# Subject residual: the run length of one of a slot's two loads, and the place of ScalarE's loop in the text

## The chip, the cores and the metric

The kernel runs on one core of one Trainium2 chip. The metric is device time in microseconds, the median of the runs of a kernel; smaller is better.

## The reference

Each of 128 samples x[b] (128 channels by 1024 steps, float32) is multiplied by the 128 by 128 matrix of its subject, one of eight, and added to itself:

```
w = weights[subjects]                      # (128, 128, 128), subjects in 0..7
out = einsum('bct,bcd->bdt', x, w)
x + out
```

x and the result have 67.1 MB each; the weights have 0.5 MB.

## The kernel before

The samples are worked in 32 turns (NT) of four: H = 2 halves of G = 2 samples. A turn has a *slot*, a piece of SBUF of 2 MB (128 partitions of 16 KB); there are 12 (SLOTS), used round robin. A slot is loaded, multiplied in place and stored from where it lies. The residual is in the weights: `place` (L193) adds the identity (`eye`) to the subject's matrix, so that one matmul gives x + out.

*Loads.* ScalarE issues two DMAs for a slot (`load`, L147), one for each half, 1 MB each. The source, two samples that lie one behind the other in HBM, is written as rows of ROWS channels: with ROWS = 8 a row is 8 x 1024 numbers, a run of 32 KB, and there are 32 of them. The destination is 128 partitions of 2048 numbers. Since source and destination are walked in the same flat order, partition p of a half gets channels 2(p mod 64) and 2(p mod 64) + 1 of sample p // 64, whatever ROWS is. Both samples of a half thus share a column range of the slot, one in the upper and one in the lower 64 partitions.

*Trades.* `trade` (L162) puts that right with three copies on ScalarE, each 64 partitions by 2048 numbers: after them each sample of the slot has all 128 partitions to itself, with two channels of it side by side in the partition order that the sorted weights and `eye` expect. The last copy of a slot raises `s_half[0]`, for which TensorE waits.

*ScalarE's loop* (L273) has AHEAD = 4 slots in a turn. For each it waits until the slot's two loads have landed (`landed`), then until a slot is empty (`s_empty`), issues the loads of the slot four ahead, and only then trades. So a trade stands behind the wait for an empty slot. Ahead of the loop ScalarE issues the loads of the first four slots (L268), loads its table and copies one element (`mark`, L271).

*Empty slots.* `s_empty` begins at SLOTS - 1 - AHEAD = 7, gets one more when the first product has been copied (the last slot holds the raw weights until then), and then one for each store that has landed, counted by GpSimd (L309).

*Multiplying.* For each half TensorE does four float32 matmuls of 128 x 128 by 512 (L206) into PSUM, VectorE copies the half back to the slot (`copy`, L221, 128 x 2048) and places the weights of the half two further on.

*Stores.* SyncE waits for VectorE's copies and stores the slot (`store`, L172), 2 MB a DMA; from slot 20 on two slots share a DMA of 4 MB. The runs of the first store are 4 KB, those of the next ones 16 KB (a partition's part of a slot), and 32 KB for the last six slots. After its last store the program ends when that has landed.

*Where the text stands.* Each engine runs its own instructions in the order in which the text gives them to it. A loop opens a new block, to which engines with work behind it branch. In the kernel before, ScalarE's loop is written ahead of the second half of the weights' sorting (VectorE and GpSimd, L293 to L305), GpSimd's counting, SyncE's stores (L311) and the loops of VectorE (L330) and TensorE (L336).

Of the kernel before, what the change touches and what calls it, by code (L numbers as in the profile page):

```python
# [30 lines left out]
G = 2  # L31
H = 2
# [3 lines left out]
SLOTS = 12  # L36
# [9 lines left out]

IDLE = 8

ROWS = 8

R = 2

AHEAD = 4

MOVES = 3
# [9 lines left out]
def transfer(nc, engine, out, in_):  # L65

    later, nc._always_lower_symbolic_ap = nc._always_lower_symbolic_ap, False
    ins, outs = engine.lower_ap_dma(in_), engine.lower_ap_dma(out)  # L70
    nc._always_lower_symbolic_ap = later
    return engine.add_instruction(
        mybir.InstDMACopy(
            name=nc.get_next_instruction_name(),
            engine=engine.engine,
            ins=ins,
            outs=outs,
            mode="Copy",
            cce_op=ALU.bypass,
            queue=QUEUES[engine.engine],  # L80
        )
    )
# [3 lines left out]
def kernel(  # L86
# [7 lines left out]
    nc = tc.nc  # L94
    B, C, T = x.shape
    S, _, D = weights.shape
    NT = B // (G * H)

    def sbuf(name, *shape, dtype=F32):
        return ctx.enter_context(nc.sbuf_tensor(name, list(shape), dtype)).ap()  # L100
# [3 lines left out]
    eye = sbuf("eye", C, 1, D)  # L104
    ws = [sbuf(f"w{i}", C, 1, D) for i in range(G)]
    mark = sbuf("mark", 1, 1)
# [32 lines left out]
    s_eye = tc.alloc_semaphore("s_eye")  # L139
    s_moved = tc.alloc_semaphore("s_moved")  # L140
    s_empty = tc.alloc_semaphore("s_empty")
    s_sort = tc.alloc_semaphore("s_sort")

    def emptied(i):
        return DMA * (i // SLOTS)

    def load(k, slot, first):  # L147
        for h in range(H):
            transfer(
                nc,  # L150
                nc.scalar,
                x_all[:, bass.ds(slot * (H * G * T) + h * G * T, G * T)],
                x[bass.ds(first + h * G, G)].rearrange("h (b r) t -> (h b) (r t)", r=ROWS),
            ).then_inc(s_in[k], DMA)

    def move(out, in_):
        nc.scalar.copy(out, in_).then_inc(s_moved, 1)  # L157

    def landed(k):
        nc.scalar.wait_ge(s_in[k], DMA * H).then_inc(s_in[k], -DMA * H)  # L160

    def trade(k, slot):  # L162
        base = slot * (H * G * T)
        both = x_all[:, bass.ds(base, H * G * T)].rearrange("c (h s t) -> c s h t", h=H, s=G)
        move(aside, both[A:, 0])
        nc.scalar.wait_ge(s_moved, k * MOVES + 1)
        move(both[A:, 0], both[:A, 1])
        nc.scalar.wait_ge(s_moved, k * MOVES + 2)
        move(both[:A, 1], aside)
        nc.scalar.wait_ge(s_moved, (k + 1) * MOVES).then_inc(s_half[0], 1)  # L170
# [52 lines left out]
    with tc.tile_critical():  # L223

        nc.sync.dma_start(
            w_raw, weights.rearrange("s (u j) d -> (s u) (j d)", j=S)
        ).then_inc(s_wall, DMA)
        nc.sync.dma_start(given, subjects.rearrange("(o b) -> o b", o=1)).then_inc(s_given, DMA)

        nc.vector.memset(zeros, 0.0).then_inc(s_zeros, 1)  # L230
        nc.tensor.wait_ge(s_zeros, 1)
        for _ in range(IDLE):
            nc.tensor.matmul(  # L233
                ps[P_SLOTS - 1][:, G - 1, :N], zeros[:, :D], zeros, start=True, stop=True
            )

        nc.vector.wait_ge(s_wall, DMA)  # L240
        for r in range(R):
            nc.vector.transpose(  # L242
                w_mid.rearrange("p (e r h w j) -> p r j h e w", e=4, r=R, h=4, w=8)[:, r],
                w_raw.rearrange("p (j r d) -> p r j d", r=R, d=D)[:, r],
            ).then_inc(s_sort, 1)
        nc.vector.memset(index[:, B:], 0).then_inc(s_index, 1)
        nc.vector.wait_ge(s_given, DMA)
        nc.vector.tensor_scalar(near, given, -S, S - 1, ALU.max, ALU.min).then_inc(s_index, 1)  # L248
        nc.vector.wait_ge(s_index, 2)
        nc.vector.tensor_scalar(wrap, near, 0, S, ALU.is_lt, ALU.mult).then_inc(s_index, 1)  # L250
        nc.vector.wait_ge(s_index, 3)
        nc.vector.tensor_tensor(index[:, :B], near, wrap, ALU.add).then_inc(s_index, 1)  # L252

        nc.gpsimd.wait_ge(s_zeros, 1)
        for r in range(R):
            if r:
                nc.gpsimd.wait_ge(s_eye, r)
            nc.gpsimd.affine_select(  # L258
                eye[:, 0],
                eye[:, 0] if r else zeros[:, :D],  # L260
                [[-1, D]],
                ALU.not_equal,
                1.0,
                base=r - r * R * A,
                channel_multiplier=R,
            ).then_inc(s_eye, 1)

        for i in range(AHEAD):  # L268
            load(i % AHEAD, i, i * (H * G))
        nc.scalar.wait_ge(s_eye, R)  # L270
        nc.scalar.copy(mark, eye[:1, 0, :1])  # L271
        nc.gpsimd.wait_ge(s_eye, R).then_inc(s_empty, SLOTS - 1 - AHEAD)
        with nc.scalar.Fori(0, NT // AHEAD) as turn:  # L273
            for k in range(AHEAD):
                landed(k)
                with nc.scalar.If(turn < NT // AHEAD - 1):
                    empty = nc.scalar.wait_ge(s_empty, k + 1)
                    if k + 1 == AHEAD:
                        empty.then_inc(s_empty, -AHEAD)
                    load(  # L280
                        k,
                        (turn * AHEAD + (k + AHEAD)) % SLOTS,
                        nc.s_assert_within(
                            turn * (AHEAD * H * G) + (k + AHEAD) * H * G,
                            0,
                            B - H * G,
                            skip_runtime_bounds_check_because="the last turn loads nothing",
                        ),
                    )
                trade(k, (turn * AHEAD + k) % SLOTS)  # L290
            nc.scalar.wait_ge(s_moved, AHEAD * MOVES).then_inc(s_moved, -AHEAD * MOVES)

        nc.vector.wait_ge(s_sort, R)  # L293
        nc.vector.transpose(w_late, w_mid).then_inc(s_sort, 1)  # L294

        def sort(engine, o, v):
            engine.tensor_copy(  # L297
                w_all[32 * v : 32 * (v + 1), 2 * o : 2 * (o + 1), :],
                w_late[32 * o : 32 * (o + 1)].rearrange(
                    "c (e u r d) -> c u r e d", e=2, u=2, r=R  # L300
                )[:, v % 2, v // 2],
            ).then_inc(s_sort, 1)

        nc.vector.wait_ge(s_sort, R + 1)
        nc.gpsimd.wait_ge(s_sort, R + 1)  # L305
        for o in range(4):
            for v in range(4):
                sort(nc.gpsimd if v == 3 else nc.vector, o, v)
        nc.gpsimd.wait_ge(s_added, 1).then_inc(s_empty, 1)  # L309
        for i in range(SLOTS, NT):  # L310
            nc.gpsimd.wait_ge(s_slot[i % SLOTS], emptied(i)).then_inc(s_empty, 1)  # L311

        for i in [*range(NT - SLOTS), *range(NT - SLOTS, NT, PAIR)]:
            n = 1 if i < NT - SLOTS else PAIR
            nc.sync.wait_ge(s_added, (i + n) * H)
            if i == 0:
                nc.sync.dma_start(
                    out[: H * G].rearrange("g d t -> d g t"), xs[0]
                ).then_inc(s_slot[0], DMA)
            elif i + n < NT:  # L320
                store(i, n).then_inc(s_slot[i % SLOTS], DMA)


        nc.vector.wait_ge(s_index, 4)
        nc.vector.wait_ge(s_sort, SORTED)
        nc.vector.wait_ge(s_eye, R)
        subject = subjects_of(slice(0, H * G))
        for h in range(H):
            place(h, subject)
        with nc.vector.Fori(0, NT // TURN) as turn:  # L330
            for n in range(TURN):
                subject = subjects_of(turn * TURN + (n + 1))
                for h in range(H):
                    copy((turn * TURN + n) % SLOTS, n, h)
                    place(h, subject)
        with nc.tensor.Fori(0, NT) as turn:  # L336
            for h in range(H):
                multiply(turn % SLOTS, h)

    with tc.tile_critical() as waits:  # L340
        for i in range(NT - SLOTS, NT - PAIR, PAIR):
            nc.scalar.wait_ge(s_slot[i % SLOTS], emptied(i + SLOTS))
    last = store(NT - PAIR, PAIR)
# [34 lines left out]
```

## Time and profile before

| | us |
|---|---|
| median of 3 runs | 322.94 |
| the three runs | 322.62 to 323.04 |
| the profiled execution | 323.06 |
| its span, first to last instruction | 321.2 |
| PE busy | 250.1 |
| ScalarE busy | 183.6 |
| VectorE busy | 181.4 |

The profiled execution agrees with the runs within 0.1 us. The profile counts DMA as packets in queues: q1 is SyncE's (the stores, the weights, the subjects), q10 is ScalarE's (the loads of x). A queue's share is the time of its packets over the 16 DMA engines' span, so the shares of the queues add up to how busy the engines were. A queue's packets include small ones under 512 B that carry nothing of x: 16 close each DMA.

### The profile page before, as it was taken

To read this page: it belongs to the slowest core of one execution; us is meant where nothing else is said; L and a number is where in the kernel's file an instruction comes from. 1 tells how busy PE (TensorE), PEld (TensorE's weight loads), DVE (VectorE), ACT (ScalarE), POOL (GpSimd) and SP (SyncE) were. 2 spreads that over 40 slices of the span, in tenths; PEclk is the share of its full clock that TensorE was granted. 3 is DMA by queue.
4 is the path that set the end of the run, shared out by engine and by line. 5 is a ranking of instruction groups with operands and counts; after the bars stand their busy time and mean duration, and the time that the engine had idled before them with its cause. 6 is when DMAs were issued, how large, how long until landed. Compare 5 with 4: busy or idle time off the path is not lost. (4 is left out here: it accounts for less than half of the span.)

```text
span 321.2 us, 2576 instructions
## 1 busy us (share of the span) xinstructions
PE 250.1 (78%) x528; PEld 103.4 (32%) x528; DVE 181.4 (56%) x217; ACT 183.6 (57%) x98; POOL 2.5 (1%) x10
## 2 busy tenths in 40 slices
PE   7479998898899885949987499673997939999400
PEld 3134433333333332413433143231433414444100
DVE  4708766666677662660865627456273753877600
ACT  1577767776777726566454774547746379990000
POOL 0200000000000000000000000000000000000000
PEclk9969999999999997995999979998697998999955
DMA  8999999999999999999999999999999999999995
GB/s 314 404 457 424 420 403 436 408 433 445 426 424 426 435 414 430 437 430 441 433 402 426 416 433 441 428 418 422 426 439 441 408 453 408 426 445 418 433 428 228
DMA packets 7732, 134.76 MB, mean 420 GB/s; under 512 B 1457, under 2 KB 1458, under 8 KB 2098
## 3 DMA queue, kind: packets, MB, share of 16 engines
q1 hardware_dynamic: 4658, 67.64, 49.9%
q10 hardware_dynamic: 3072, 67.11, 49.0%
q14 instruction: 2, 0.02, 0.0%
HBM read 67.63 MB, written 67.11 MB: 419 GB/s over the span
## 5 line engine op out<-in xcount | busy, mean ns | idle before, releaser
L206 PE MATMUL ps<-x_all,w 128*128 x512 | 239.9, 627 | 48.7 <-PEq L202 48.7
L221 DVE COPY x_all<-ps 128x2048 f32 x64 | 146.6, 2291 | 116.1 <-PE ps L206 103.5
L206 PEld LDWEIGHTS ps<-x_all,w 128*128 128x128 f32 x512 | 99.3, 200 | 189.3 <-issue 189.2
L157 ACT COPY aside<-x_all 64x2048 f32 x32 | 60.7, 1897 | 95.0 <-issue 90.6
L157 ACT COPY x_all<-x_all x32 | 60.7, 1897 | 4.0
L157 ACT COPY x_all<-aside 64x2048 f32 x32 | 60.7, 1898 | 1.0
L195 DVE TENSOR_TENSOR w<-w_all,eye 128x128 f32<-128x128 f32 x132 | 31.8, 282 | 0.8 <-issue 0.8
L233 PE MATMUL ps<-x_all 128*128 128x512 f32 x16 | 10.2, 808 | 1.7 <-DVE x_all L230 1.7
L233 PEld LDWEIGHTS ps<-x_all 128*128 128x128 f32 x16 | 4.1, 262 | 6.9 <-issue 5.3
L271 ACT ACT_TABLE_LOAD x1 | 1.3, 1283 | 6.1 <-issue 6.1
L297 DVE COPY w_all<-x_all 32x256 f32<-32x256 f32 x12 | 3.9, 326 | 0.4
L242 DVE STREAM_TRANSPOSE x_all<-x_all 128x512 f32<-128x512 f32 x2 | 2.0, 1068 | 3.2 <-DMA x_all<-in_L_cond_weights_dram 3.2
L297 POOL COPY w_all<-x_all 32x256 f32<-32x256 f32 x4 | 1.7, 424 | 6.7 <-DVE x_all L294 6.6
L294 DVE STREAM_TRANSPOSE x_all<-x_all 128x1024 f32<-128x1024 f32 x1 | 1.2, 1226 | 0.0
L230 DVE MEMSET x_all<- 128x512 f32 x1 | 0.5, 485 | 1.0 <-SPq L223 1.0
L248 DVE TENSOR_SCALAR x_all<-x_all 1x128 int32<-1x128 int32 x1 | 0.2, 217 | 0.3 <-DMA x_all<-in_itok_B_dram 0.3
L258 POOL TENSOR_SCALAR_AFFINE_SELECT eye<-x_all 128x128 f32<-128x128 f32 x1 | 0.3, 292 | 1.4 <-DVE x_all L230 1.4
L252 DVE CUSTOM_DVE_ANT_0 index<-x_all 1x256 uint16<-1x256 uint16 x1 | 0.3, 280 | 0.0
L258 POOL TENSOR_SCALAR_AFFINE_SELECT eye<-eye 128x128 f32<-128x128 f32 x1 | 0.3, 292 | 0.1
L250 DVE TENSOR_SCALAR x_all<-x_all 1x128 int32<-1x128 int32 x1 | 0.2, 215 | 0.0
L271 ACT COPY mark<-eye 1x1 f32<-1x1 f32 x1 | 0.2, 190 | 0.0
L365 POOL MEMSET const-bfloat16-1.0<- 128x1 bf16 x1 | 0.1, 100 | 0.0
(5 smaller groups left out, 0.4 us busy)
## 6 DMA issues: line engine op xcount, KB each, us to landing
x_all<-in_x_dram ACTq DMA_DIRECT2D x64, 1024.0 KB, 11.6
out_dram<-x_all SPq DMA_DIRECT2D x20, 2048.0 KB, 55.0
out_dram<-x_all SPq DMA_DIRECT2D x6, 4096.0 KB, 30.9
x_all<-in_L_cond_weights_dram SPq DMA_DIRECT2D x1, 512.0 KB, 3.9
x_all<-in_itok_B_dram SPq DMA_DIRECT2D x1, 0.5 KB
```

The source lines that it names most:

```text
L157: nc.scalar.copy(out, in_).then_inc(s_moved, 1)
L195: copy = nc.vector.tensor_tensor(ws[q], w_all[:, bass.ds(subject[q], 1), :], eye, ALU.add)
L206: mm = nc.tensor.matmul(ps[h][:, q % G, t : t + N], ws[q][:, 0, :], x_all[:, bass.ds(at, N)], start=True, stop=True,)
L221: nc.vector.tensor_copy(mine, ps[h].rearrange("d g t -> d (g t)")).then_inc(s_added, 1)
L230: nc.vector.memset(zeros, 0.0).then_inc(s_zeros, 1)
L233: nc.tensor.matmul(ps[P_SLOTS - 1][:, G - 1, :N], zeros[:, :D], zeros, start=True, stop=True)
L242: nc.vector.transpose(w_mid.rearrange("p (e r h w j) -> p r j h e w", e=4, r=R, h=4, w=8)[:, r], w_raw.rearrange("p (j r d) -> p r j d", r ...
L252: nc.vector.tensor_tensor(index[:, :B], near, wrap, ALU.add).then_inc(s_index, 1)
L258: nc.gpsimd.affine_select(eye[:, 0], eye[:, 0] if r else zeros[:, :D], [[-1, D]], ALU.not_equal, 1.0, base=r - r * R * A, channel_multipli ...
L271: nc.scalar.copy(mark, eye[:1, 0, :1])
L294: nc.vector.transpose(w_late, w_mid).then_inc(s_sort, 1)
L297: engine.tensor_copy(w_all[32 * v : 32 * (v + 1), 2 * o : 2 * (o + 1), :], w_late[32 * o : 32 * (o + 1)].rearrange("c (e u r d) -> c u r e ...
```

## The change

Two edits. First, ROWS becomes a list: the load of the first half of a slot is written as 64 rows of 4 channels (16 KB runs), that of the second half as 32 rows of 8 channels (32 KB runs), as both were. Bytes, destinations, issue order and semaphores are as before.

Second, what ScalarE does after the first loads (its wait for `eye`, the copy of `mark`, its loop) is written last, behind the rest of the sorting, GpSimd's counting, SyncE's stores and the loops of VectorE and TensorE. No other line changes.

```
-ROWS = 8
+ROWS = [4, 8]
...
-                x[bass.ds(first + h * G, G)].rearrange("h (b r) t -> (h b) (r t)", r=ROWS),
+                x[bass.ds(first + h * G, G)].rearrange("h (b r) t -> (h b) (r t)", r=ROWS[h]),
             ).then_inc(s_in[k], DMA)
...
         for i in range(AHEAD):
             load(i % AHEAD, i, i * (H * G))
+        nc.gpsimd.wait_ge(s_eye, R).then_inc(s_empty, SLOTS - 1 - AHEAD)
+        nc.vector.wait_ge(s_sort, R)
+        nc.vector.transpose(w_late, w_mid).then_inc(s_sort, 1)
...
+        with nc.tensor.Fori(0, NT) as turn:
+            for h in range(H):
+                multiply(turn % SLOTS, h)
+
         nc.scalar.wait_ge(s_eye, R)
         nc.scalar.copy(mark, eye[:1, 0, :1])
-        nc.gpsimd.wait_ge(s_eye, R).then_inc(s_empty, SLOTS - 1 - AHEAD)
         with nc.scalar.Fori(0, NT // AHEAD) as turn:
             for k in range(AHEAD):
                 landed(k)
```

What the second edit moves is seen in the order of each engine's instructions. On ScalarE (ACT), from its start to the first loads of the loop; `L72` are the loads, `mark` is the one element copied after the table load:

```order
 L374 UNCONDITIONAL_BRANCH x2
 L72 DMA x_all<-in_x_dram 128x2048 x8
-L271 ACT_TABLE_LOAD
-L271 COPY mark<-eye 1x1
-L273 UNCONDITIONAL_BRANCH
-L276 COMPARE_AND_BRANCH
+L225 UNCONDITIONAL_BRANCH
+L319 ACT_TABLE_LOAD
+L319 COPY mark<-eye 1x1
+L320 UNCONDITIONAL_BRANCH
+L323 COMPARE_AND_BRANCH
 L70 ISA x2
```

A branch to the block with the loop stands ahead of the table load now; the rest of ScalarE's instructions keep their order, under other line numbers.

On VectorE (DVE), between the subjects' index and the sorting of the weights:

```order
 L250 TENSOR_SCALAR x_all<-x_all 1x128
 L252 ISA index<-x_all 1x256
-L225 UNCONDITIONAL_BRANCH
-L294 STREAM_TRANSPOSE x_all<-x_all 128x1024
-L297 COPY w_all<-x_all 32x256 x12
+L272 STREAM_TRANSPOSE x_all<-x_all 128x1024
+L275 COPY w_all<-x_all 32x256 x12
 L184 TENSOR_LOAD index
```

The branch ahead of the transposition is gone.

On SyncE (SP), from the load of the subjects to the last but one store:

```order
 L228 DMA x_all<-in_itok_B_7_dram 1x128
-L225 UNCONDITIONAL_BRANCH
-L317 DMA out_dram<-x_all 128x4x1024
+L295 DMA out_dram<-x_all 128x4x1024
 L72 DMA out_dram<-x_all 128x4x1024 x19
 L72 DMA out_dram<-x_all 128x8x1024 x5
-L293 UNCONDITIONAL_BRANCH
+L225 UNCONDITIONAL_BRANCH
```

Of its two branches the one ahead of the stores is gone, and one behind them stays.

More of the change, by code (lines that the diff above doesn't have):

```diff
@@ L269 @@
             load(i % AHEAD, i, i * (H * G))
-        nc.scalar.wait_ge(s_eye, R)
-        nc.scalar.copy(mark, eye[:1, 0, :1])
         nc.gpsimd.wait_ge(s_eye, R).then_inc(s_empty, SLOTS - 1 - AHEAD)
[L273 to L291, printed above, removed]
         nc.vector.wait_ge(s_sort, R)
@@ L338 @@
                 multiply(turn % SLOTS, h)
+        nc.scalar.wait_ge(s_eye, R)
+        nc.scalar.copy(mark, eye[:1, 0, :1])
+        with nc.scalar.Fori(0, NT // AHEAD) as turn:
+            for k in range(AHEAD):
+                landed(k)
+                with nc.scalar.If(turn < NT // AHEAD - 1):
+                    empty = nc.scalar.wait_ge(s_empty, k + 1)
+                    if k + 1 == AHEAD:
+                        empty.then_inc(s_empty, -AHEAD)
+                    load(
+                        k,
+                        (turn * AHEAD + (k + AHEAD)) % SLOTS,
+                        nc.s_assert_within(
+                            turn * (AHEAD * H * G) + (k + AHEAD) * H * G,
+                            0,
+                            B - H * G,
+                            skip_runtime_bounds_check_because="the last turn loads nothing",
+                        ),
+                    )
+                trade(k, (turn * AHEAD + k) % SLOTS)
+            nc.scalar.wait_ge(s_moved, AHEAD * MOVES).then_inc(s_moved, -AHEAD * MOVES)
     with tc.tile_critical() as waits:
```

## The prediction

> **What bounds the kernel now.** I read the page's head and its DMA rows first, because the kernel reads and writes all of x once and computes little. The rows are the span, the DMA engines' busy share in 40 slices, the bytes moved, and the two queues (q10 carries the loads that ScalarE issues, q1 carries SyncE's stores and the two small loads at the start).
>
> ```profile
> span 321.2 us, 2576 instructions
> PE 250.1 (78%) x528; PEld 103.4 (32%) x528; DVE 181.4 (56%) x217; ACT 183.6 (57%) x98; POOL 2.5 (1%) x10
> DMA  8999999999999999999999999999999999999995
> GB/s 314 404 457 424 420 403 436 408 433 445 426 424 426 435 414 430 437 430 441 433 402 426 416 433 441 428 418 422 426 439 441 408 453 408 426 445 418 433 428 228
> DMA packets 7732, 134.76 MB, mean 420 GB/s; under 512 B 1457, under 2 KB 1458, under 8 KB 2098
> q1 hardware_dynamic: 4658, 67.64, 49.9%
> q10 hardware_dynamic: 3072, 67.11, 49.0%
> ```
>
> Packets take 49.9% + 49.0% = 98.9% of 16 engines' span, 317.7 of 321.2 us. No compute engine comes near that (PE 78%). So the DMA engines are the bound from the first slice to the last, and a wait between compute engines is worth nothing unless it leaves both queues empty. Next I read stretches of the span, and in three of them the queues' own rows: 10 to 28 us has only loads, 270 to 288 us only stores in 16 KB runs, 291 to 316 us only stores in 32 KB runs. The last two columns of the first fence are DMA share and GB/s.
>
> ```profile
> 10.00:28.00 18.00, 12.14 (x25) 5.02 (x24) 7.84 (x18) 12.57 (x7) 0.91 (x3) 0.81 1.01 435
> 30.00:56.00 26.00, 24.42 (x57) 10.15 (x56) 18.84 (x21) 18.83 (x11) 0.00 (x0) 1.00 1.00 415
> 56.00:116.00 60.00, 54.11 (x122) 22.52 (x122) 40.35 (x45) 40.72 (x22) 0.00 (x0) 1.00 1.00 429
> 116.00:268.00 152.00, 116.61 (x238) 47.87 (x237) 80.72 (x90) 88.55 (x47) 0.00 (x0) 0.91 1.00 427
> 270.00:288.00 18.00, 18.00 (x43) 7.62 (x42) 14.11 (x16) 15.93 (x10) 0.00 (x0) 1.00 1.00 424
> ```
>
> ```profile
> DMA packets 351, 7.83 MB, mean 435 GB/s; under 512 B 112, under 2 KB 112, under 8 KB 112
> q10 hardware_dynamic: 351, 7.83, 101.2%
> ```
>
> ```profile
> DMA packets 483, 7.64 MB, mean 424 GB/s; under 512 B 17, under 2 KB 17, under 8 KB 17
> q1 hardware_dynamic: 483, 7.64, 99.8%
> ```
>
> ```profile
> DMA packets 360, 10.75 MB, mean 430 GB/s; under 512 B 32, under 2 KB 32, under 8 KB 32
> q1 hardware_dynamic: 360, 10.75, 100.8%
> out_dram<-x_all SPq DMA_DIRECT2D x1, 4096.0 KB, 16.5
> ```
>
> The share is 1.00 in every stretch. Taking the packets under 512 B away (they carry no data of x), a 32 KB load packet takes 1.012 x 16 x 18 us / 239 = 1219.5 ns, a 16 KB store packet 0.998 x 288 us / 466 = 616.8 ns, a 32 KB store packet 1.008 x 400 us / 328 = 1229.3 ns. One packet split in two costs 2 x 616.8 - 1229.3 = 4.3 ns more.
>
> **Part 1, the 16 KB runs.** A load now has 32 packets of 32 KB; the first load of each slot gets 64 of 16 KB. That is 32 slots x 32 = 1024 packets more, 64 for each of 16 engines. No row shows a 16 KB load, so I bound its price. The nearest row is the split of a store: 64 x 4.3 ns = 0.28 us. The far row is what a load packet costs beyond its 1219.5 ns when stores run beside it, over the long middle and, without pauses of the loads, over its first part (60 to 260 us, then 60 to 100 us):
>
> ```profile
> q10 hardware_dynamic: 2040, 44.34, 51.9%
> q1 hardware_dynamic: 2824, 41.29, 48.7%
> ```
>
> ```profile
> q10 hardware_dynamic: 475, 10.36, 60.4%
> q1 hardware_dynamic: 472, 6.95, 40.8%
> ```
>
> 44.34 MB are 1353 packets, and 0.519 x 3200 us / 1353 = 1227.5 ns, 8.0 ns over. If every added packet met that as well, it would be 64 x (4.3 + 8.0) = 0.79 us. From below I can't exclude a gain, which the next step prices. I take 0.28 us, since it is the same size of packet on the same engines, and keep 0.79 us for the range.
>
> The Trainium skill, page DMA: Bandwidth & Descriptors, section Why small descriptors are slow (HBM only), gives a fixed cost of about 3 cycles a packet; at the 850 MHz of its section Where 436 GB/s comes from I estimate 3.5 ns, and by that the sum would be 64 x 3.5 = 0.23 us, without the far end. The trace agrees for stores alone (4.3 ns) and not for loads beside stores (8.0 ns over).
>
> **What the runs do to the two queues' shares.** Two places: 221 to 227 us, where both queues have work, and 176 to 180 us.
>
> ```profile
> q10 hardware_dynamic: 61, 1.47, 57.4%
> q1 hardware_dynamic: 61, 0.98, 38.5%
> ```
>
> ```profile
> q1 hardware_dynamic: 105, 1.70, 100.2%
> q10 hardware_dynamic: 16, 0.00, 0.2%
> ```
>
> 61 packets and 61: the queues take turns, packet by packet, the small closing packets counted too. By that, while both have work, the loads of a slot take 6 turns of each engine now (2 x (2 + 1)), and 8 after (4 + 1 + 2 + 1). A slot's load data are 4 x 1.2195 = 4.88 us of each engine; a store turn is on average 8 x 0.617 / 9 = 0.55 us. So a slot's loads pass in 4.88 + 6 x 0.55 = 8.2 us now and in 4.88 + 8 x 0.55 = 9.3 us after, while the whole kernel needs 4.88 + 4.93 = 9.8 us a slot. Now loads run 1.6 us a slot ahead, use up the empty slots and stop: 60.4% of the time from 60 to 100 us, 51.9% over 60 to 260 us, nothing at 176 us. After, they run 0.5 us ahead; their share should be about 4.88 / 9.3 = 53% early and stay there, and most pauses go. Since the engines are busy with stores in the pauses, this moves no work off the bound by itself. What it can save is what packets lose when the loads restart: from 60 to 100 us a load packet takes 0.604 x 640 us / 316 = 1223.3 ns, over the whole middle 1227.5. The 4.2 ns between them are 1353 x 4.2 / 16 = 0.36 us an engine. I take all of it as gone: -0.36 us (none of it, if restarts stay).
>
> The same page's section Queues, rings and completion order says that an engine drains a packet of some 9 to 17 descriptors before it turns to another queue. If a run were only one of those descriptors, its length would leave the turns alone, and the pauses and the 0.36 us would stay; the 61 to 61 with runs of 32 and 16 KB speaks for one run to a turn.
>
> **The end.** The last packets are not level over the engines. Windows at the end (share and GB/s last; a packet is counted where it begins):
>
> ```profile
> 317.00:317.60 0.60, 0.00 (x0) 0.00 (x0) 0.00 (x0) 0.00 (x0) 0.00 (x0) 0.50 0.77 328
> 317.60:318.20 0.60, 0.00 (x0) 0.00 (x0) 0.00 (x0) 0.00 (x0) 0.00 (x0) 0.50 0.01 0
> 318.20:318.80 0.60, 0.00 (x0) 0.00 (x0) 0.00 (x0) 0.00 (x0) 0.00 (x0) 0.50 0.13 55
> 318.60:318.70 0.10, 0.00 (x0) 0.00 (x0) 0.00 (x0) 0.00 (x0) 0.00 (x0) 0.50 0.77 328
> 318.70:321.20 2.50, 0.00 (x0) 0.00 (x0) 0.00 (x0) 0.00 (x0) 0.00 (x0) 0.50 0.00 0
> ```
>
> 0.77 x 0.1 us x 16 = 1.23 us is one 32 KB packet, and 0.13 x 0.6 us x 16 = 1.25 us says that it is the only one to begin between 318.2 and 318.8. It begins after 318.6 us, when the others have begun their last by 317.6: one engine is at least 1.0 us behind, and the program waits for it. Each engine has the same packets to move, so its lag is gathered from delays like those of the restarts. With fewer of them I take 0.3 us of that lag as gone, a choice between 0 and 1.0 us.
>
> **Part 2, ScalarE's loop written later.** Its instructions are the same, with one branch more ahead of the table load; VectorE, GpSimd and SyncE lose one at the start, and SyncE's other one comes after its stores. ScalarE's first rows:
>
> ```profile
> 6.08 1.28 ACT L271 ACT_TABLE_LOAD   x1 [6.08 <-issue]
> 7.38 0.19 ACT L271 COPY mark<-eye 1x1 f32<-1x1 f32 x1
> 10.14 1.16 ACTq L72 DMA_DIRECT2D x_all<-in_x_dram  x2
> 11.47 1.90 ACT L157 COPY aside<-x_all 64x2048 f32 x1 [3.91 <-issue]
> ```
>
> A branch and a wait between the issue's end (11.30) and the copy (11.47) take 0.17 us, so one branch costs at most that. It would delay the fifth slot's loads, issued at 10.14 us. They have cover: eight loads (8.39 MB) stand in the queue before, the first slice moved 314 GB/s x 8.03 us = 2.52 MB with 0.52 MB of weights in it (8 x 128 x 128 numbers of 4 bytes), and the remaining 6.4 MB at 435 GB/s last until 22.7 us. With the cover gone it would cost its 0.17 us once. I take 0.
>
> **The tail's cover.** The last store's row above says 16.5 us from issue to landing, and its 4.19 MB take 9.8 us at 430 GB/s; so up to 6.7 us of other stores stand ahead of it, and compute may be that late before a queue runs empty. The last trades wait for the store that frees the last slot, as now, and with more load bytes still open at that moment the cover grows rather than shrinks. I take 0.
>
> **Sum.** +0.28 - 0.36 - 0.3 + 0 + 0 = -0.4 us. The profiled execution took 323.06 us (span 321.2 and 1.9 around it), which becomes 322.7; it stands 0.1 us over the median of the three runs, 322.94, so against that I say 322.5 us.
>
> **The rivals.** About 0.2% (0.65 us) is what a measurement of this kernel can tell from no change, so faster means under 322.3 and slower over 323.6.
>
> *Faster: the late engine catches up.* If the restarts made the lag, and they go, the whole 1.0 us goes with the 0.36: 0.28 - 0.36 - 1.0 = -1.1, so 321.8 us. For it speaks that only one engine is late and that the shares come out so near to balance (9.3 against 9.8 us); against it, that no view names the engine or when it fell behind.
>
> *Slower: 16 KB loads beside stores pay per packet.* With the turns more even, loads and stores alternate all the time, and a 16 KB load packet may lose as much at each turn as a 32 KB one: 0.79 us with no gain at the end, 323.7 us. It decides from 0.65 us / 64 = 10 ns an added packet. For it: the 8.0 ns. Against: 3.8 ns in the stretch without pauses, so that half of it belongs to restarts.
>
> *No split at all.* If adjoining runs are joined again below the kernel's text, the packets and the time stay, 322.9 us. Against it: the present 32 KB runs adjoin too, and are packets of their own.
>
> **How the numbers follow.** My forecast (bound unchanged, small terms that nearly cancel) 0.45, by its own bounds 322.3 to 323.2; the late engine catching up 0.37; the per-packet loss 0.14; no split 0.04. That gives faster 0.37, same 0.49, slower 0.14. The range reaches to both far cases, 321.6 (the faster rival with the packets free) to 323.8.
>
> **What would show it.** The loads' queue should have 4096 packets in place of 3072; its share from 60 to 100 us about 53% where it was 60.4%, and no stretch of a few us between 60 and 260 us without loads; DMA share 1.00 in each stretch. At the end, one packet still beginning over 0.6 us after the others says that the lag stayed. I am wrong if the DMA share falls below 0.98 anywhere between 10 and 316 us, if the last store's 16.5 us come down to its own 9.8 us, or if 16 KB load packets take over 620 ns.

## The result, and the profile after

| | before | changed |
|---|---|---|
| median of 22 runs | 322.96 us | 322.19 us |
| lowest to highest | 322.11 to 323.42 us | 321.68 to 322.92 us |
| profiled execution, its span | 323.06, 321.2 us | 321.88, 320.1 us |

The ratio is 0.9979, its 95% interval 0.9971 to 0.9986: faster by 0.45 to 0.94 us. (Medians are of all runs; the ratios, here and below, leave out disturbed runs, so that a ratio and its medians can differ.) The forecast was 322.5, and 321.6 to 323.8 was the range. So the time lies in the range, but 0.1 us outside the forecast's own bounds (322.3 to 323.2); by the mark that the prediction set, under 322.3, it counts as faster, to which it gave 0.37, and 0.49 to the same time as before.

The page of the changed kernel, the rows that answer to those of before (span, DMA share in slices, packets, the two queues):

```profile
span 320.1 us, 2576 instructions
DMA  8999999999999999999999999999999999999996
DMA packets 8757, 134.76 MB, mean 421 GB/s; under 512 B 1458, under 2 KB 1459, under 8 KB 2099
q1 hardware_dynamic: 4658, 67.64, 49.9%
q10 hardware_dynamic: 4096, 67.11, 49.2%
x_all<-in_x_dram ACTq DMA_DIRECT2D x64, 1024.0 KB, 15.2
```

The loads' queue has the 4096 packets that the split was to give, and a load now takes 15.2 us from issue to landing at the median. The engines are as full as before: 99.1% of 320.1 us are 317.2 us of packets, where they were 317.7. What the packets leave of the span went from 3.5 to 2.9 us. The queues' rows of the changed kernel at 60 to 100, 60 to 260, 221 to 227 and 176 to 180 us:

```profile
q10 hardware_dynamic: 554, 8.88, 51.9%
q1 hardware_dynamic: 563, 8.18, 48.0%
```

```profile
q10 hardware_dynamic: 2750, 44.86, 52.4%
q1 hardware_dynamic: 2791, 40.75, 47.9%
```

```profile
q10 hardware_dynamic: 75, 1.47, 57.4%
q1 hardware_dynamic: 74, 1.10, 43.0%
```

```profile
q10 hardware_dynamic: 58, 1.20, 69.8%
q1 hardware_dynamic: 52, 0.67, 39.6%
```

The loads have 51.9% early and 52.4% over the whole middle, where they had 60.4 and 51.9: they no longer run ahead, and where they stood still (176 us) they are at work. 75 packets beside 74 say that the queues still move as many packets each. That they alternate one by one is seen in the order of the packets: in the trace an engine's next packet begins some 3 ns before the one ahead of it ends. From 60 to 100 us, 953 of the 1117 packets have exactly one such successor, and all 953 hand over to the other queue.

The end of the changed kernel, windows of 0.2 us (DMA share and GB/s last), and the row of its last store:

```profile
316.40:316.60 0.20, 0.00 (x0) 0.00 (x0) 0.00 (x0) 0.00 (x0) 0.00 (x0) 0.50 2.69 1147
316.60:316.80 0.20, 0.00 (x0) 0.00 (x0) 0.00 (x0) 0.00 (x0) 0.00 (x0) 0.50 0.38 164
317.00:317.20 0.20, 0.00 (x0) 0.00 (x0) 0.00 (x0) 0.00 (x0) 0.00 (x0) 0.50 0.38 164
317.20:317.40 0.20, 0.00 (x0) 0.00 (x0) 0.00 (x0) 0.00 (x0) 0.00 (x0) 0.50 0.01 0
317.40:317.60 0.20, 0.00 (x0) 0.00 (x0) 0.00 (x0) 0.00 (x0) 0.00 (x0) 0.50 0.39 164
```

```profile
out_dram<-x_all SPq DMA_DIRECT2D x1, 4096.0 KB, 20.2
```

One engine begins its last packet (0.39 x 0.2 us x 16 = 1.25 us, one of 32 KB) 0.2 to 0.6 us after the one before it, where it was 1.0 us or more. The last store lands 20.2 us after its issue, where it was 16.5: there is more cover at the end, not less.

### The profile page after: what moved, and what is told of

The parts are those of the page before. It is cut to its first block, busy times and chain, and to the rows that moved or that the text cites. A ratio compares the mean times of both kernels' runs of the same rounds, so it can differ in the third digit from the quotient of the medians.

```text
span 320.1 us, 2576 instructions
## 1 busy us (share of the span) xinstructions
PE 246.2 (77%) x528; PEld 101.7 (32%) x528; DVE 181.3 (57%) x217; ACT 183.6 (57%) x98; POOL 2.5 (1%) x10
## 3 DMA queue, kind: packets, MB, share of 16 engines
q1 hardware_dynamic: 4658, 67.64, 49.9%
q10 hardware_dynamic: 4096, 67.11, 49.2%
## 5 line engine op out<-in xcount | busy, mean ns | idle before, releaser
L206 PE MATMUL ps<-x_all,w 128*128 x512 | 236.6, 619 | 47.9 <-PEq L202 47.9
L206 PEld LDWEIGHTS ps<-x_all,w 128*128 128x128 f32 x512 | 97.8, 196 | 186.6 <-issue 186.5
## 6 DMA issues: line engine op xcount, KB each, us to landing
x_all<-in_x_dram ACTq DMA_DIRECT2D x64, 1024.0 KB, 15.2
```

Source lines behind the costliest of these rows:

```text
L206: mm = nc.tensor.matmul(ps[h][:, q % G, t : t + N], ws[q][:, 0, :], x_all[:, bass.ds(at, N)], start=True, stop=True,)
```

## The experiments

Each kernel was timed beside the kernel before on the same chip. "Pauses" are stretches in which the loads' queue stands still; "turns" are packets of one queue that an engine takes, each followed by one of the other.

| run | turns a slot, loads pause? | median, us | ratio to before (95%) |
|---|---|---|---|
| changed | 8, no | 322.19 | 0.9979 (0.9971 to 0.9986) |
| e1 run lengths alone | 8, no | 322.00 | 0.9969 (0.9959 to 0.9979) |
| e2 loop alone | 6, yes | 322.66 | 0.9996 (0.9983 to 1.0008) |
| e3 half of the early stores longer | 6, in part | 323.57 | 1.0023 (1.0000 to 1.0046) |
| e4 both loads 16 KB | 10, no | 332.17 | 1.0270 (1.0237 to 1.0303) |
| e5 four loads a slot | 8, no | 344.93 | 1.0654 (1.0612 to 1.0696) |
| e6 stores in 8 KB | 8, yes | 323.48 | 1.0019 (1.0008 to 1.0030) |
| e7 last two slots stored singly | 6, yes | 322.82 | 1.0005 (0.9992 to 1.0018) |
| e8 = e3 and e7 | 6, in part | 324.45 | 1.0028 (1.0001 to 1.0056) |
| e9 one tiny DMA a slot | 8, no | 323.49 | 1.0029 (1.0011 to 1.0047) |
| e10 two tiny DMAs a slot | 10, no | 338.52 | 1.0314 (1.0291 to 1.0338) |
| e11 the changed kernel again | 8, no | 321.86 | 0.9971 (0.9959 to 0.9983) |
| e12 = e9, more 32 KB stores | 8, no | 323.75 | 1.0035 (1.0019 to 1.0051) |

**e1 and e2: which of the two edits.** Each is made alone, e1 on the kernel before, e2 on the changed one:

```
-ROWS = 8
+ROWS = [4, 8]
...
-                x[bass.ds(first + h * G, G)].rearrange("h (b r) t -> (h b) (r t)", r=ROWS),
+                x[bass.ds(first + h * G, G)].rearrange("h (b r) t -> (h b) (r t)", r=ROWS[h]),
```

```
-ROWS = [4, 8]
+ROWS = [8, 8]
```

> Only the run lengths are changed (16 KB and 32 KB); ScalarE's loop stands where it stood before. If the runs are the cause (turns: 8 a slot in place of 6, the loads no longer pause): ratio to the kernel before 0.997 to 0.9985, the loads' share from 60 to 100 us near 52%, no pause at 176 us. If the place of the loop is the cause: ratio 0.9995 to 1.0005.

> Only ScalarE's loop is written last; both loads in 32 KB runs. If the runs are the cause: ratio 0.9995 to 1.0005, the loads' share from 60 to 100 us 60% and their pauses back. If the place of the loop is the cause: ratio 0.997 to 0.9985.

The run lengths alone give the whole gain (0.9969), the loop alone nothing that can be told (0.9996). The queues of e1 from 60 to 260 us, then those of e2 from 60 to 100 us and at 196 to 200 us:

```profile
q10 hardware_dynamic: 2752, 44.83, 52.4%
q1 hardware_dynamic: 2794, 40.80, 48.0%
```

```profile
q10 hardware_dynamic: 469, 10.36, 60.4%
q1 hardware_dynamic: 473, 6.96, 40.9%
```

```profile
q1 hardware_dynamic: 111, 1.74, 102.2%
q10 hardware_dynamic: 3, 0.00, 0.0%
```

e1 has the changed kernel's shares, e2 those of the kernel before, with a pause at 196 us.

**e4: both loads in 16 KB.** `ROWS = [4, 4]` in the changed kernel.

> Both loads in 16 KB runs, the loop written last. 10 turns a slot: its loads pass in 4.88 + 10 x 0.55 = 10.4 us, more than the 9.8 us that a slot needs. If only the pauses count: no pauses, 64 packets more an engine than the changed kernel (+0.28 us), ratio to the kernel before 0.998 to 0.9995. If finer packets are the cause: faster than the changed kernel, ratio 0.996 to 0.9975. If the loads come so late that the end loses its cover: they end near 290 us in place of 266, the last store lands in its own 10 to 12 us, and the ratio is 1.000 to 1.005.

The third case came, at five times the price that I had set for its worst (2.7% for 0.5%). The queues of e4 from 60 to 100 us, stretches of its end (busy times, then DMA share and GB/s), and what its engines do there:

```profile
q1 hardware_dynamic: 623, 9.00, 52.9%
q10 hardware_dynamic: 616, 8.14, 47.7%
```

```profile
300.00:307.00 7.00, 0.80 (x3) 0.22 (x2) 2.75 (x4) 5.69 (x3) 0.00 (x0) 0.92 1.04 445
310.00:320.00 10.00, 6.83 (x13) 2.52 (x11) 5.38 (x6) 0.00 (x0) 0.00 (x0) 0.84 0.00 0
320.00:332.60 12.60, 0.00 (x0) 0.00 (x0) 0.00 (x0) 0.00 (x0) 0.00 (x0) 0.50 0.78 333
```

```profile
300.56 1.90 ACT L157 COPY aside<-x_all 64x2048 f32 x1 [9.18 <-ACTq L160]
306.79 10.04 PE L206 MATMUL ps<-x_all,w 128*128 x16 [6.20 <-PEq L202]
317.08 2.29 DVE L221 COPY x_all<-ps 128x2048 f32 x1 [0.79 <-DVEq L218]
320.07 0.56 SPq L72 DMA_DIRECT2D out_dram<-x_all  x1
```

The loads fall behind the stores, and ScalarE stands 9.18 us until the last ones have landed. The last slot is then traded, multiplied and copied while the DMA engines stand still from 310 to 320 us, and the last 4 MB go alone. Two turns a slot more than the changed kernel, and the bound breaks open at the end.

**e9 and e10: turns without 16 KB packets.** In the kernel before, behind the two loads of a slot, EXTRA = 1 or 2 loads of 16 x 512 bytes into an unused place:

```
...
+        for j in range(EXTRA):
+            transfer(
+                nc,
+                nc.scalar,
+                extra[:, (k * EXTRA + j) * D : (k * EXTRA + j + 1) * D],
+                x[bass.ds(first, 1), :DMA, :D].rearrange("h c t -> (h c) t"),
+            ).then_inc(s_in[k], DMA)
...
```

> The kernel before (all runs 32 KB, the loop as before), and behind a slot's two loads one more DMA of 16 x 512 bytes into an unused place: one small packet and one closing packet an engine, 2 turns. 4 + 2 + 2 = 8 turns a slot, as in the changed kernel, with no 16 KB packet of x. If turns and pauses are the cause: the loads' share from 60 to 100 us near 53%, no pause at 176 us, ratio to the kernel before 0.996 to 0.998, as the changed kernel or up to 0.2 us faster. If it is the 16 KB packets themselves: ratio 0.9995 to 1.001.

> As the run before, with two tiny DMAs a slot: 10 turns, as with both loads in 16 KB runs. If turns alone set the queues' shares: a slot's loads pass in 4.88 + 10 x 0.55 = 10.4 us, the loads end near 299 us, the last store waits for compute with empty queues, and the ratio is 1.015 to 1.035. If the 2.7% of the run with 16 KB packets came from the packets: ratio 0.999 to 1.002.

e10 shows that it is turns: 0.5 MB of tiny DMAs cost 3.1%, 10 us, most of it by an end like that of e4. (In the profiled execution packets take 97.2% of 329.5 us, 320.3, some 2.6 us more than before; the rest of its loss is idle queues.) e10 from 60 to 100 us, and two stretches of its end:

```profile
q1 hardware_dynamic: 622, 9.14, 53.9%
q10 hardware_dynamic: 622, 7.90, 46.8%
```

```profile
314.00:318.00 4.00, 0.00 (x0) 0.00 (x0) 2.69 (x3) 0.00 (x0) 0.00 (x0) 0.76 0.00 0
318.00:329.50 11.50, 0.00 (x0) 0.00 (x0) 0.00 (x0) 0.00 (x0) 0.00 (x0) 0.50 0.85 365
```

622 packets stand against 622, and the loads' share is 46.8%, as e4 has with 16 KB runs. (The profiled execution, 331.3 us, is the quickest of six that reach to 346.)

e9 has the shares and no gain. Its loads have 52.7% from 60 to 100 us and 39.2% at 176 us, so the pauses are gone; yet it is 0.4 to 1.5 us slower than before. Its page, and its end:

```profile
q1 hardware_dynamic: 4658, 67.64, 49.5%
q10 hardware_dynamic: 4096, 67.38, 49.2%
```

```profile
318.00:318.20 0.20, 0.00 (x0) 0.00 (x0) 0.00 (x0) 0.00 (x0) 0.00 (x0) 0.50 0.40 164
318.20:318.40 0.20, 0.00 (x0) 0.00 (x0) 0.00 (x0) 0.00 (x0) 0.00 (x0) 0.50 0.00 0
319.20:319.40 0.20, 0.00 (x0) 0.00 (x0) 0.00 (x0) 0.00 (x0) 0.00 (x0) 0.50 0.38 164
```

Its loads' queue is busy 49.2% of 321.9 us, 158.4 us an engine, where the kernel before has 49.0% of 321.2, 157.4: the 64 small packets an engine cost a net 1.0 us, more than the gain in question, which my expectation had left out. And one engine begins its last packet at least 1.0 us after the one before it (318.2 to 319.2) here too, without pauses. The time fits neither case of my expectation. So e9 doesn't show the gain, nor that it needs the 16 KB packets; but its stores' queue, with the same 4658 packets, took 159.3 us (49.5% of 321.9) where it took 160.3 before (e2 and e7: 159.8 and 159.9), so that this part of the gain may be there without them.

**e6: 16 KB loads with pauses.** e1, with the stores up to slot 25 in 8 KB runs:

```
-                "d (o t) -> d o t", o=1 if i >= NT - WHOLE else n
+                "d (o t) -> d o t", o=1 if i >= NT - WHOLE else 2 * n
```

> The changed kernel's 16 and 32 KB loads, the loop as before, and the stores up to slot 25 in 8 KB runs. A store's turn is 16 x 0.31 / 17 = 0.29 us, so a slot's loads pass in 4.88 + 8 x 0.29 = 7.2 us and the pauses are longer than in the kernel before. About 200 packets more an engine than the changed kernel, 0.86 us at 4.3 ns. If the pauses are the cause: pauses in the profile, a late engine at the end, 1.2 to 2 us over the changed kernel, ratio 1.001 to 1.004. If fine packets level the engines: only the 0.86 us, ratio 0.999 to 1.001, and a level end.

The ratio is the one forecast for the pauses (1.0019), but not for that reason alone. The queues of e6 over its whole page, from 60 to 100 us, from 246 to 248 us, and its end:

```profile
q1 hardware_dynamic: 7858, 67.64, 50.1%
q10 hardware_dynamic: 4096, 67.11, 49.1%
```

```profile
q10 hardware_dynamic: 655, 10.49, 61.3%
q1 hardware_dynamic: 861, 6.66, 39.5%
```

```profile
q1 hardware_dynamic: 104, 0.84, 100.3%
```

```profile
318.20:318.40 0.20, 0.00 (x0) 0.00 (x0) 0.00 (x0) 0.00 (x0) 0.00 (x0) 0.50 0.77 328
318.40:319.00 0.60, 0.00 (x0) 0.00 (x0) 0.00 (x0) 0.00 (x0) 0.00 (x0) 0.50 0.00 0
319.20:319.40 0.20, 0.00 (x0) 0.00 (x0) 0.00 (x0) 0.00 (x0) 0.00 (x0) 0.50 0.39 164
```

With the very loads of e1, shorter store turns bring back the 60%, the pauses, and an engine that is at least 0.8 us late. Its stores' queue takes 50.1% of 321.9 us where the changed kernel has 49.9% of 320.1: 1.5 us for 200 packets an engine. That alone is the loss against e1 (323.48 - 322.00 = 1.5 us), so the times don't separate the two. The end doesn't either: one engine is late, but what the packets leave of the span is 321.9 x 0.8% = 2.6 us, no more than in the changed kernel. What does separate them are single packets. From 60 to 260 us, 99 packets of e6 take over 30 ns longer than the median of their queue and size, 98 of them at the end of a pause, and that costs 0.62 us an engine; e1, with the same loads and no pauses, has none. So the pauses have a price of their own, and most of the rest is the finer stores (200 x 6.1 ns = 1.2 us, by the durations of 8 and 16 KB store packets that run alone).

**e3: longer store turns, 32 KB loads.** In the kernel before, the stores of slots 2 and 3, 6 and 7 and so on up to 18 and 19 share a DMA of 32 KB runs:

```
...
-            n = 1 if i < NT - SLOTS else PAIR
+            n = 1 if i < NT - SLOTS and i % 4 != 2 else PAIR
...
```

> The loads as before (32 KB), the loop as before; half of the early stores go two slots at a time in 32 KB runs, so that the stores' turns are longer: 9 turns of 1.09 us for two slots beside 18 of 0.55, 0.73 us on average, and a slot's loads should pass in 4.88 + 6 x 0.73 = 9.3 us, as in the changed kernel. If the pauses of the loads are the cause: no pauses, a level end, and 40 packets an engine fewer than before (-0.17 us): ratio 0.996 to 0.998, as fast as the changed kernel or 0.1 to 0.4 us faster. If it is the fineness of the 16 KB load packets that levels the end: ratio 0.9995 to 1.0, since packets only get coarser here.

Missed: 1.0023. The share from 60 to 100 us is 52.0%, as meant, but a pair frees two slots at once, so that it swings: 39.8% from 110 to 120 us, 61.1% from 140 to 150 us. An average in balance isn't enough. Its executions reach to 326.4 us, for which I suspected the end.

**e7 and e8: cover at the end.** Slots 30 and 31 are stored one by one, in the kernel before (e7) and in e3 (e8):

```
...
-    last = store(NT - PAIR, PAIR)
+    last = store(NT - 1, 1)
...
```

> The kernel before with the last two slots stored one by one instead of in one DMA; the last store then needs only 4.9 us alone, 4.9 us more cover. If the changed kernel gains because its last store is issued earlier (more cover at the end): ratio 0.997 to 0.9985 here too. If pauses and the late engine are the cause: ratio 0.9995 to 1.0005.

> The mixed stores of the third run with the last two slots stored one by one. If its executions of 324 to 326 us come from an end without cover: they go, the median falls from 323.6 to 322.2 to 322.8, ratio 0.998 to 0.9995. If they come from the pauses: the median stays over 323.2.

More cover changes nothing (1.0005), so that the changed kernel's 20.2 us in place of 16.5 are no part of its gain. e8 stays over 323.2 us as well: the executions of over 324 us in e3 don't come from an uncovered end. Nor do they come from the pauses: the profile of e8 is of such an execution (324.57 us), and from 60 to 260 us it has one pause of over 1 us, yet 81 slow packets worth 1.2 us an engine, 6 of them near that pause. What makes them is open.

**e5: four loads a slot.** In the kernel before, a load for each sample, to 64 partitions, in place of one for two:

```
-        for h in range(H):
+        for q in range(H * G):
...
+                    q % G * A : (q % G + 1) * A,
...
```

> The loop as before and all runs 32 KB as before, but each slot is loaded by four DMAs of one sample instead of two of two samples, so that four small packets close them in place of two: 8 turns of an engine a slot, as in the changed kernel, without its 64 added data packets. If turns and pauses are the cause: the loads' share from 60 to 100 us near 53%, no pause at 176 us, ratio to the kernel before 0.996 to 0.998, and up to 0.28 us faster than the changed kernel. If fine 16 KB packets are the cause: ratio 0.9995 to 1.001 (twice as many issues on ScalarE, some 1.2 us a slot, off the bound).

No test of the question: the loads that run alone at the start have half the rate. e5 from 10 to 40 us:

```profile
DMA packets 416, 6.82 MB, mean 227 GB/s; under 512 B 208, under 2 KB 208, under 8 KB 208
```

From 60 to 260 us, loads and stores together move 429 GB/s as in the other runs. The loads' share from 60 to 100 us is 60.6%, not the 53% of my expectation: part of the first store, with its 4 KB runs, passes there. From 100 to 140 us it is 52.4%, as 8 turns a slot should give.

**e11 and e12.** The changed kernel beside e9 and e10, and e9 with `WHOLE = 12`.

> The changed kernel itself, beside the two runs before on the same chip: ratio 0.997 to 0.9985, as its own runs and the run lengths alone gave.

> The run with one tiny DMA, and the stores of slots 20 to 25 in 32 KB runs as well (24 packets an engine fewer, 0.1 us at 4.3 ns). If packet costs are what is left: 0.1 us faster than with one tiny DMA alone, which this measurement can hardly tell. Where those stores meet the last loads, their turns are longer: the loads of the last slots come up to 2 us later, under cover.

e11 repeats the gain (0.9971). e12 (323.75 us) can't be told from e9. No version beat the changed kernel beyond doubt.

## Why the prediction was right or wrong

*The bound.* Right: DMA share 1.00 or near it in every stretch, in both kernels, and the edit that left the DMA packets as they were (e2) did not move the time.

*Part 1, the price of the split.* From 10 to 28 us the changed kernel's loads run alone:

```profile
DMA packets 464, 7.86 MB, mean 437 GB/s; under 512 B 112, under 2 KB 112, under 8 KB 112
q10 hardware_dynamic: 464, 7.86, 101.8%
```

7.86 MB are 239.9 runs of 32 KB, moved in 352 packets and 1.018 x 288 = 293.2 us; at 1219.5 ns that would have been 292.6 without a split. The 112 packets more cost 0.64 us, 5.7 ns each, but the last digits of the share and of the 7.86 MB are worth 1 to 2 ns each here. The traces hold every packet's own duration, which is sharper. Beside stores (60 to 260 us of the changed kernel) a 16 KB load packet takes 612.0 ns on average and a 32 KB one 1218.8, so a split costs 5.2 ns; for loads alone (10 to 28 us) it is 611.0 and 1213.0, so 9.0 ns. Most of the loads run beside stores: some 64 x 5.2 = 0.33 us an engine, where I took 0.28 and kept 0.79. The 3.5 ns that I estimated from the Trainium skill's page (DMA: Bandwidth & Descriptors, section Why small descriptors are slow) is under all of these. My 1219.5 ns was a little high: I took the closing packets out of the count but not their 9 ns each out of the time, and without them it is 1214.8.

*The shares.* Right, and shown from several sides: turns of single packets, the small closing ones too. 8 turns gave 51.9% where 53 was forecast (the changed kernel; e9 with other packets: 52.7%), 10 turns 47.7 and 46.8% (e4, e10), shorter store turns brought 61.3% back (e6). My argument from 61 packets to 61 was too weak: turns of several packets, as many for each queue, would give the same counts and the same shares. The order settles it, with all 953 links from one queue to the other. By the Trainium skill (DMA: Bandwidth & Descriptors, section Queues, rings and completion order) a turn is a packet of typically some 9 to 17 descriptors. The trace doesn't show such turns here: one run, or one closing packet, is a turn.

*The restarts.* Right in kind, and now seen directly. I took 0.36 us, from load packets alone. From 60 to 260 us, take the packets that last over 30 ns longer than the median of their queue and size, and add up their excess. The three profiles with 6 turns (before, e2, e7) have 50, 56 and 64 of them, worth 0.44, 0.38 and 0.57 us an engine; three with the 16 KB runs (the changed kernel, e1, e11) have 2, 0 and 2, worth 0.01 us or less. Of the 50, 56 and 64, 46, 43 and 58 begin near the end of a pause of over 1 us (0.7 us ahead of it to 2.5 behind, some 35 of the 200 us). Only about half of the excess is in loads (0.27, 0.18 and 0.28 us). The rest is in the stores, which I hadn't priced. The rows agree: the stores' queue took 160.3 us an engine before (49.9% of 321.2) and 159.7 after (49.9% of 320.1), while the loads' queue, with 64 packets more, went from 157.4 to 157.5.

*The end.* Here the size was off, and it is the term that makes up most of what I missed. I let 0.3 us of the late engine's lag go, "a choice between 0 and 1.0 us"; it was no derived number, so how near the forecast came is partly luck. What the packets leave of the span, summed from the packets themselves, is 3.7, 3.6 and 3.6 us in the three with 6 turns and 2.9, 2.9 and 3.0 in the other three: some 0.66 us. So the sum, 0.33 - 0.46 - 0.66 = -0.8 us, agrees with the -0.8 us of the medians, where I had 0.28 - 0.36 - 0.3. The time fell about midway between my forecast and the rival with the late engine.

*Why an engine is late* isn't settled. I had put it down to restarts, and they are not the whole of it. The last packet of all begins 1.2, 1.1 and 0.6 us after the one before it in the three with 6 turns, and 0.3, 0.7 and 0.5 us in the other three, so that the two groups overlap. What the packets leave of the span goes with the run length of the loads rather than with the pauses: 2.6 us in e6, with 16 KB runs and pauses; 3.5 in e5, 3.8 in e12 and 4.0 in e9, with 32 KB runs and hardly a pause. And when the last engine of the kernel before is followed back from packet to packet (by the nearest link where several fit), it was already 1.3 us behind the median engine at 40 us, ahead of the first pause at 52 us, and 1.8 us at the end; the one of e9 was 1.5 behind at 40 us and 1.9 at the end. In e7 the lag did grow with the pauses, from 0.1 us at 57 us to 1.4. These are single profiles, and in e9 and e12 the tiny DMAs may play a part, in e5 the loads to 64 partitions. No run separated the finer packets from the rest of what happens at the start.

*Part 2 and the cover.* Right: nothing for the loop (e2). The cover grew, as I wrote; how much hung on it I did not see. e4 lost it with two turns a slot more, at 9 us.

*The slower rival,* a loss per packet at each turn, is out: 5.2 ns beside stores, and 10 were needed.

*No split at all* is out by the 4096 packets.

## What to carry to other kernels

In this kernel the DMA engines are the bound and two queues share them; run length sets who gets how much, since the queues take turns by packets. Where that is so, the same reckoning can be tried. Work out the time that a unit's loads take in turns (data + turns x the other queue's mean turn) and set it a little under what a unit needs in all: here 9.3 us against 9.8. Well under it (8.2) cost 0.2%, over it (10.4) cost 2.7%, so err on the side of loads that come too early. Two runs warn: an average in balance isn't enough (e3), and small DMAs added for their turns cost more than they gain (e9).

## What the runs showed of the hardware

- With two queues at work, a DMA engine took one packet of each in turn, a run of 16 or 32 KB being one packet: all 953 links that can be followed in the changed kernel from 60 to 100 us.
- The closing packet of a DMA takes a turn like a packet of data: 622 against 622 with tiny DMAs in the queue (e10), and 0.5 MB of such loads cost 3.1%.
- Packets of both queues were slower where the loads set in again after a pause: 0.38 to 0.57 us an engine in the three profiles with 6 turns, 0.62 in e6, 0.01 or less in the three with 8 turns and 16 KB runs.
- Loads to 64 partitions each, alone on the engines, moved 227 GB/s (e5) where loads to 128 moved 435. The Trainium skill, page SBUF — State Buffer, section Door 1: The DMA port swizzle, says that bandwidth depends on how many of 16 ports the partitions reach, and 64 in a row reach half of them; the 227 agrees. Beside stores the same packets were not slow: 0.546 x 3200 us / 1423 = 1.23 us each from 60 to 260 us, where they took 1.014 x 480 us / 208 = 2.34 us alone. No run shows why.
- A packet more costs, by the packets' own durations, 4.8 ns (stores alone, 32 to 16 KB), 5.2 ns (loads beside stores, 32 to 16 KB), 9.0 ns (loads alone, 32 to 16 KB) or 6.1 ns (stores alone, 16 to 8 KB, e6).
